# A message-passing layer: the last quad's statistics, weights and scatter taken pair by pair, and its update split three pairs to one

## The chip, the cores and the metric

The kernel runs on one core of one Trainium2 chip. The metric is device time in microseconds of one execution. Before the change the median of four runs was 577.39 us, from 576.52 to 577.80.

## The reference

One layer of a graph network on 128 graphs of 64 nodes with 128 features. Every ordered pair of nodes has a message, a three-layer network with layer norms; the messages are masked by the adjacency matrix and summed; a second network of the same form updates the node.

```python
def _mlp(x, w0, b0, g0, be0, w1, b1, g1, be1, w2, b2):
    h = relu(x @ w0 + b0);  h = _layernorm(h, g0, be0)
    h = relu(h @ w1 + b1);  h = _layernorm(h, g1, be1)
    return h @ w2 + b2
# x: (128, 64, 128), adj: (128, 64, 64) of 0 and 1, about one entry in eight set
pair_feats = concatenate([f_i, f_j], axis=-1)            # (B, P, P, 2C)
messages   = _mlp(pair_feats, msg_*) * adj[..., None]
agg        = sum(messages, axis=2)
out        = x + _mlp(concatenate([x, agg], axis=-1), upd_*)
```

## The kernel before, in words

**Edges, not node pairs.** Only the edges that the adjacency matrix has are computed. Two graphs are a *pair* (64 of them, `NP`); a pair has 2 x 640 edge slots, 10 tiles of 128 edges. Two pairs are a *quad* (32, `NQ`; 20 tiles, `QT`), and four tiles are a *chunk*, so a quad has 5 chunks (`QC`) and the whole 160 (`NCHK`). Four pairs are a *block* (16, `NB`) of 512 nodes, the unit of the node update. The last quad, 31, holds pairs 62 and 63 and chunks 155 to 159; the last block, 15, holds pairs 60 to 63, and block 14 pairs 56 to 59.

**A chunk.** `layer0` forms h on TensorE (PE) and ScalarE (ACT). `stats0` turns h on PE and takes `bn_stats` on VectorE (DVE). Layer norms are not applied to the data: their means are folded into the weights and their deviations are carried as per-edge factors. `layer1` (eight steps later, `L1`) multiplies h by the centred weights onto a bias scaled by the deviation and leaves y = relu(...) by ACT. `stats1` takes the statistics of y on DVE.

**A quad.** `var1_step` combines the statistics of 20 tiles (seven small instructions: on GpSimd, POOL, and on DVE for the last quad), `root1_of` takes the root on ACT, `inverse_of` the reciprocal on DVE. `weights(p, g)` multiplies a pair's edge-to-node marks by this factor (two instructions a pair, on POOL; for the last quad pair 62's are on DVE). `reduce(p)` is the scatter: ten products y x weights on PE that sum a pair's edges into its nodes, in the PSUM bank `ys`. In the last block the bank is taken anew for its second half.

**A block.** A `Unit` is the update of some pairs of a block. It copies the sums (`sums_out`, ysum), turns and copies them (`turn`, `turn_out`, ysumT), multiplies (`layer`), adds the bias `m0` of `bias0` and takes relu with statistics (`layer_out`, uh), turns and copies that, multiplies by u1 and adds `usdb`, the bias scaled by the deviation (`upd_shift`, one ACT instruction a pair), takes uy, turns, multiplies by u2, and ends with `finish`, one DVE instruction `uo` a pair and a store. Variances are `upd_m0` and `upd_m1`, five and seven small instructions, by POOL or by DVE. Up to block 14 a block is one unit. Block 15 is two: pairs 60, 61 and pairs 62, 63. All units' tiles of one name share one buffer (`bufs=1`), `uo`, `xo` and `m0` two.

**Order.** Every engine works through its own queue in the order in which the program issues. That order is written by hand: `at(n, place, fn, ...)` puts a call into step n at a place, and the last loop runs, for each step, the places "a", "m", then `layer1(n - 8)`, "b", `layer0`, `stats0`, "k", `stats1(n - 8)`, "x", "x1", "x2", "e0", "e1", "e". `LAST` lists the steps of the units of the last blocks. Steps of the tail: `layer1` of chunk 155 is in step 163, of chunk 159 in 167; the last scatter is in step 169.

**Lines.** L249 to L278 are the small statistics, roots and reciprocals; L567 the split of a root; L609 and L612 `layer1`; L619 `stats1`; L682 `weights`; L695 `reduce`; L721 ysum; L728 `bias0`; L734 `residual` (xo); L740 and L745 turning and copying out; L754 the units' products; L242 and L764 uh, uy and their statistics; L777 `upd_shift`; L791 uo; L794 the store.

Of the kernel before, what the change touches and what calls it, by code (L numbers as in the profile page):

```python
# [23 lines left out]
def tile_gnn(  # L24
# [245 lines left out]
    def root1(stp, v, n, name):  # L270

        sq = stp.tile([P, n], F32, name=name + "_sq")
        nc.scalar.activation(sq, v, AF.Sqrt, scale=1.0 / C, bias=eps2_c)
        return sq
# [14 lines left out]
    def edge_path(es):  # L289
# [3 lines left out]
        sp = es.enter_context(tc.tile_pool(name="sp", bufs=4))  # L293
        hp = es.enter_context(tc.tile_pool(name="hp", bufs=9))
        yp = es.enter_context(tc.tile_pool(name="yp", bufs=12))
        lp = es.enter_context(tc.tile_pool(name="lp", bufs=3))
        wp = es.enter_context(tc.tile_pool(name="wp", bufs=2))
        updp = es.enter_context(tc.tile_pool(name="upd", bufs=1))
        stp = es.enter_context(tc.tile_pool(name="stp", bufs=5))
# [22 lines left out]
        def zbank(k):  # L322
            return ps_z[k].tile([P, CH * C], F32, name=f"z{k}")
# [4 lines left out]
        def at(n, place, fn, *args):  # L328
            plan.setdefault((n, place), []).append((fn, args))
# [284 lines left out]
        def stats1(n):  # L614
# [3 lines left out]
            for t in range(CH):  # L618
                nc.vector.bn_stats(ST1[q][:, CH * c + t, :], Y[n][:, t, :])  # L619

        def var1_step(q):
            Q[q] = var1_of(stp, ST1.pop(q), V0.pop(q), QT, "m21", eng_of(q))

# [18 lines left out]
        def bias_table():  # L642

            K = 4 * QT
            part, tile_of = W.pop("part"), W["tile_of"]
            hi = const.tile([P, C], F32R, name="b1hi")
            nc.scalar.copy(hi, W["b1b"])
            lo = const.tile([P, C], F32, name="b1lo")
            nc.gpsimd.tensor_tensor(lo, W["b1b"], hi.bitcast(F32), op=ALU.subtract)
            nc.gpsimd.tensor_scalar(lo, lo, part[:, 1:2], None, op0=ALU.mult)  # L650
            mix = const.tile([P, C], F32, name="b1mix")
            nc.gpsimd.tensor_scalar(mix, hi.bitcast(F32), part[:, 0:1], None, op0=ALU.mult)
            nc.gpsimd.tensor_tensor(mix, mix, lo, op=ALU.add)
            W["b1t"] = const.tile([K, QT, C], F32R, name="b1t")
            W["b1mix"], W["tile_of"] = mix[0:K], tile_of[0:K]
# [20 lines left out]
        def weights(p, g):  # L676

            q, h = divmod(p, 2)
            if g == 0:
                WT[p] = wp.tile([P, TG, 2, N], F32, name="w")  # L680
            k = (2 * h + g) * TG
            (nc.vector if p == NP - 2 else nc.gpsimd).tensor_tensor(  # L682
                WT[p][:, :, g, :], OH[p][:, :, g * N:(g + 1) * N],
                Q[q][:, k:k + TG].unsqueeze(2).to_broadcast([P, TG, N]), op=ALU.mult)

        def reduce(p):
            b, k = divmod(p, PB)
            if k == 0 or (b == NB - 1 and k == PB // 2):
                YS[b] = ps_y.tile([P, PB, C], F32, name="ys")
            w = WT.pop(p)  # L690
            for t in range(TG):
                for g in range(2):
                    tile_no = p * 2 * TG + g * TG + t
                    y = Y[tile_no // CH][:, tile_no % CH, :]
                    nc.tensor.matmul(YS[b][g * N:(g + 1) * N, k, :], lhsT=w[:, t, g, :], rhs=y,  # L695
                                     start=(t == 0), stop=(t == TG - 1))
            if p % 2:
                for n in range(p // 2 * QC, (p // 2 + 1) * QC):
                    del Y[n]
# [12 lines left out]
        def wide(name, u):  # L712

            if name not in u.blk:
                u.blk[name] = updp.tile([P, PB, C], F32, name=name,
                                        bufs=2 if name in ("uo", "xo", "m0") else 1)
            return u.blk[name][:, u.q, :]

        def sums_out(u):
            u.ysum = wide("ysum", u)  # L720
            nc.scalar.copy(u.ysum, YS[u.b][:, u.q, :])  # L721
            if u.k0 + u.n == PB:
                del YS[u.b]

        def bias0(u):
            u.m0 = wide("m0", u)
# [46 lines left out]
        def upd_shift(u, q0, q1):  # L773
            if q0 == 0:
                u.usdb = wide("usdb", u)
            for q in range(q0, q1):
                nc.scalar.activation(u.usdb[:, q, :], W["bu1b"], AF.Copy, scale=u.sd[:, q:q + 1])  # L777

# [9 lines left out]
        def finish(u):  # L788
            o = wide("uo", u)
            for q in range(u.n):  # L790
# [16 lines left out]

        LAST = ((1, 2, 3, 3, 4, 5, 6, 6, 8, 9, 10, 11, 11, 11, 12),
                (0, 5, 6, 6, 7, 7, 8, 8, 8, 9, 9, 10, 10, 10, 11),
                (2, 2, 3, 3, 4, 4, 5, 5, 5, 6, 6, 7, 7, 7, 8),  # L810
                (1, 1, 2, 2, 3, 3, 4, 4, 4, 5, 5, 6, 6, 6, 7))
        for b in range(NB):
            o = b * CPB
# [19 lines left out]
        for b in reversed(range(NB)):  # L833
            o = b * CPB
            n = o + QC + SC

            if b < NB - 1:
                t = STEADY if b < NB - 3 else LAST[b - NB + 3]
                units = [(Unit(b, 0, PB, nc.gpsimd, ubank), n, t, 0, t[5] - 1)]
                if b == NB - 2:  # L840
                    units = [units[0][:3] + (-5, -4)]
            else:
                units = [(Unit(b, 2, 2, nc.vector, lambda: zbank(1), tbank), NCHK + L1 + 1, LAST[3], 1, 1),
                         (Unit(b, 0, 2, nc.gpsimd, lambda: zbank(0), hbank), NCHK + L1 - 1, LAST[2], 3, 3)]
            for u, n, t, m0_at, xo_at in units:
                at(n + m0_at, "m", bias0, u)
                at(n + xo_at, "e", residual, u)
                at(n + t[0], "a", sums_out, u)
                at(n + t[1], "x", turn, u, "ysum")
                at(n + t[2], "a", turn_out, u, "ysum")  # L850
                at(n + t[3], "x", lambda u: layer(u, ("xn", u0a), ("ysumT", W["w2u"])), u)
                at(n + t[4], "m", layer_out, u, "uh", "m0")
                at(n + t[4], "e", upd_m0, u)
                at(n + t[5], "x", turn, u, "uh")
                at(n + t[6], "a", turn_out, u, "uh")
                at(n + t[7], "a", upd_root0, u)
                if t is STEADY:
                    for k, q0, q1 in ((0, 0, 1), (1, 1, 2), (2, 2, PB)):
                        at(n + t[7] + k, "x", upd_shift, u, q0, q1)
                else:  # L860
                    at(n + t[7], "x", upd_shift, u, 0, u.n)
                at(n + t[8], "x", lambda u: layer(u, ("uhT", W["u1c"])), u)
                at(n + t[9], "m", layer_out, u, "uy", "usdb")
                at(n + t[9], "e", upd_m1, u)
                at(n + t[10], "x", turn, u, "uy")
                at(n + t[11], "a", turn_out, u, "uy")
                at(n + t[12], "a", upd_root1, u)
                at(n + t[12], "m", upd_inverse, u)
                at(n + t[13], "x", lambda u: layer(u, ("uyT", W["u2c"])), u)
                at(n + t[14], "m", finish, u)  # L870
        for p in range(NP):
            n = p * TG * 2 // CH
            if p > 1:
                if p > 2:
                    at(max(n - 7, p - 2), "a", distance, p)
                    at(max(n - 6, p - 2), "m", make_tp, p)
                at(n - 5, "a", node_rows, p)
                at(n - 4, "a", stack, p, 0, IR)
                for k in range(2):
                    at(n - 5 + k, "k", marks, p, k)  # L880
                    at(n - 5 + k, "k", compare, p, k)
                at(n - 3, "a", stack, p, 1, JR)
            w = p // 2 * QC + QC + L1 + p % 2
            last = p // 2 == NQ - 1
            at(w - 4, "a", node_marks, p)
            q, h = divmod(p, 2)
            for g in range(2):
                wait = h + 2 if q == NQ - 3 else h + 1 if q == NQ - 2 else 2 + (2 * h + g + 1) // 2
                at(*((NCHK + L1, "b") if last else (q * QC + QC + L1 + wait, "e1")), weights, p, g)
            at(NCHK + L1 + 1 if last else q * QC + SC - (q >= NQ - 3), "x1", reduce, p)  # L890
        for q in range(NQ):
            n = q * QC + QC if q else LEAD
            last = q == NQ - 1
            end = q * QC + QC + L1
            at(n, "e0", var0_of, q)
            at(*((n, "e1") if last else (n + 1, "b")), root_of, q)
            at(*((n + 2, "b") if last else (n + 1 if q else QC + 1, "x")), turn_root, q)
            at(n + 2 if q else QC + 2, "x" if last else "a", root_out, q)
            at(end - last, "e1", var1_step, q)
            wait = 0 if last else 1 if q == NQ - 2 else 2  # L900
            at(end + wait, "a", root1_of, q)
            at(end + wait, "m", inverse_of, q)


        for n in range(2, NCHK - L1):
# [304 lines left out]
```

## Time and profile before

| | |
|---|---|
| median of four runs | 577.39 us |
| the profiled execution | 577.28 us, span 575.5 us |
| granted TensorE clock, mean | 0.995 |
| PE busy | 550.2 us (96%) |
| DVE, ACT, POOL busy | 479.8, 476.8, 339.4 us |
| last y (chunk 159) ends on ACT | 550.92 us |
| last scatter ends on PE | 558.37 us |
| last uo ends on DVE | 571.53 us |

The profile is of one execution. A row of the timeline has the start in us from the span's start, the duration, the engine, the line, the operation, the tile written and the tiles read, and in brackets the idle time before it and what ended that. A row with "x4" is four instructions merged, and its duration runs from the first's start to the last's end. In the waits, the numbers are the total in us, how often, and the longest. In the windows, the first two numbers are the stretch and its length; then come the busy times of PE, PE's weight loads, DVE, ACT and POOL, the granted clock, the DMA share and GB/s. Matmuls with fp32 data are recorded as two instructions each, and their ends are modelled.

### The profile page before, as it was taken

The numbers are of one execution on the slowest core, as the hardware profiler recorded it, in microseconds if no ns is written. First come the engines' busy times: TensorE is split into PE (matmuls) and PEld (weight loads), VectorE is DVE, ScalarE is ACT, GpSimd is POOL, SyncE is SP. The second block draws the span as 40 slices with busy tenths as digits, with TensorE's granted clock in tenths as the row PEclk, the third lists the DMA queues.
The fourth block names the chain that finished last, engine by engine and source line by source line (L and its number), as shares of the span: only waits on it lengthen the run. The fifth ranks groups of instructions, "written<-read, shape, count | busy, mean of one in ns | idle before, by whom it ended". The sixth has DMA issues, their size and how long they took to land. (4 is left out here: it accounts for less than half of the span.)

```text
span 575.5 us, 15748 instructions
## 1 busy us (share of the span) xinstructions
PE 550.2 (96%) x5303; PEld 515.5 (90%) x5303; DVE 479.8 (83%) x1944; ACT 476.8 (83%) x1149; POOL 339.4 (59%) x898
## 2 busy tenths in 40 slices
PE   7798999999999999999999999999999999998894
PEld 5587889999999999999999999999999999988883
DVE  5768789797989989798989979798988979896686
ACT  5677979898888989898888989888898989886434
POOL 3344466665767666565767656575766656556342
PEclk9989999999999999999999999999999999999999
DMA  4454545365544555468454555555376564631201
GB/s 101 102 136 106 127 104 139 87 120 133 125 129 104 141 113 127 103 116 153 107 138 91 134 116 117 130 125 130 93 147 113 125 104 103 134 93 32 34 21 40
DMA packets 90770, 63.21 MB, mean 110 GB/s; under 512 B 57399, under 2 KB 74813, under 8 KB 90685
## 3 DMA queue, kind: packets, MB, share of 16 engines
q1 hardware_dynamic: 90396, 62.03, 48.4%
q8 instruction: 43, 0.70, 0.5%
q14 instruction: 43, 0.34, 0.2%
q10 hardware_dynamic: 288, 0.13, 0.1%
HBM read 6.82 MB, written 4.19 MB: 19 GB/s over the span
## 5 line engine op out<-in xcount | busy, mean ns | idle before, releaser
L552 DVE BATCH_NORM_STATS2 st<-hT 128x6 f32<-128x128 f32 x640 | 142.1, 285 | 36.6 <-PE hT L548 35.1
L609 PE MATMUL z<-w1c,h 128*128 128x128 f32 x1280 | 172.2, 277 | 0.0
L609 PEld LDWEIGHTS z<-w1c,h 128*128 128x128 f32 x1280 | 161.0, 192 | 8.2 <-issue 5.1
L597 ACT ACTIVATE z<-b1b,m_sd 128x128 f32<-128x128 f32 x360 | 133.5, 371 | 8.7
L619 DVE BATCH_NORM_STATS2 st<-y 128x6 f32<-128x128 f32 x640 | 137.7, 278 | 2.7 <-ACT y L612 1.4
L612 ACT ACTIVATE y<-z 128x512 f32<-128x512 f32 x160 | 94.5, 591 | 26.7 <-PE z L609 24.9
L542 ACT ACTIVATE h<-hps,b0c 128x512 f32<-128x512 f32 x160 | 109.4, 684 | 4.6 <-PE hps L539 4.4
L548 PE MATMUL hT<-ident,h 128*128 128x128 f32 x640 | 98.2, 276 | 1.6 <-DVE st L552 1.5
L682 POOL TENSOR_TENSOR w<-oh,m_q 128x320 f32<-128x320 f16 x126 | 91.9, 741 | 9.9 <-PE hT L548 5.3
L539 PE MATMUL hps<-s,abl 128*128 128x512 f32 (+3 forms) x256 | 93.5, 377 | 1.5 <-ACT h L542 0.8
L548 PEld LDWEIGHTS hT<-ident,h 128*128 128x128 f32 x640 | 76.9, 142 | 11.9 <-ACT h L542 1.3
L497 POOL CAST i<-tp 128x640 fp32r<-128x640 f16 x58 | 41.7, 718 | 66.6 <-DVE tp L488 48.7
L539 PE MATMUL hps<-s,abh 128*128 128x512 f32 (+3 forms) x256 | 79.7, 330 | 0.0
L695 PE MATMUL ys<-y,w 128*64 128x128 f32 x1280 | 76.9, 275 | 0.0
L695 PEld LDWEIGHTS ys<-y,w 128*64 128x64 f32 x1280 | 69.2, 137 | 4.2 <-issue 3.6
L249 POOL TENSOR_TENSOR m_d<-st 128x20 f32<-128x20 f32 x62 | 16.3, 262 | 91.0 <-DVE st L552 78.0
L521 DVE TENSOR_TENSOR j<-mk,cmpt 128x320 fp32r<-128x320 f32 x124 | 58.8, 474 | 3.0 <-PE mk L513 3.0
L539 PEld LDWEIGHTS hps<-s,abl 128*128 128x128 f32 x256 | 50.3, 196 | 3.6 <-ACT h L542 2.1
L482 ACT ACTIVATE d<-slot,mid 128x640 f16<-128x640 f16 x64 | 52.7, 823 | 0.0
L539 PEld LDWEIGHTS hps<-s,abh 128*128 128x128 f32 x256 | 50.5, 197 | 0.0
L473 DVE TENSOR_TENSOR abl<-mu,abh 128x512 fp32r<-128x512 f32 (+1 forms) x33 | 22.3, 675 | 31.6 <-ACT abh L467 31.1
L513 PE MATMUL mk<-tp,posall 128*128 128x320 f16 x126 | 38.3, 304 | 3.1 <-POOL posall L397 2.5
(224 smaller groups left out, 980.8 us busy)
## 6 DMA issues: line engine op xcount, KB each, us to landing
s<-i SPq DMA_DIRECT2D x124, 160.0 KB, 2.7
s<-j SPq DMA_DIRECT2D x124, 160.0 KB, 2.6
xn<-in_x_dram SPq DMA_DIRECT2D x15, 256.0 KB, 3.6
out_dram<-uo SPq DMA_DIRECT2D x15, 256.0 KB, 2.4
an<-in_adj_dram SPq DMA_DIRECT2D x16, 128.0 KB, 2.6
oh<-tp SPq DMA_TRANSPOSE x64, 3.3
xn<-in_x_dram SPq DMA_DIRECT2D x2, 128.0 KB
out_dram<-uo SPq DMA_DIRECT2D x2, 128.0 KB, 2.6
```

Of the source, the lines that this page charges most:

```text
L482: nc.scalar.activation(D[p], slot, AF.Abs, bias=blocks[b]["mid"][:, q:q + 1], scale=-1.0)
L521: nc.vector.tensor_tensor(JR[p][:, c], MK.pop((p, k))[:, 0:HC], cmpt[:, c], op=ALU.is_equal)
L539: nc.tensor.matmul(ps[:, c:c + w], lhsT=ab[:, g % 4, :], rhs=s, start=(k == 0), stop=(k == 1))
L542: nc.scalar.activation(H[n], ps, AF.Relu, bias=b0c)
L548: nc.tensor.transpose(ps[:, t, :], H[n][:, t * P:(t + 1) * P], ident)
L552: nc.vector.bn_stats(ST0[q][:, CH * c + t, :], ps[:, t, :])
L597: nc.scalar.activation(Z[n][:, t, :], W["b1b"], AF.Copy, scale=SR[q][:, k:k + 1])
L609: nc.tensor.matmul(ps[:, t, :], lhsT=h[:, t * P:(t + 1) * P], rhs=W["w1c"], start=False, stop=True, skip_group_check=True)
L612: nc.scalar.activation(Y[n], ps, AF.Relu)
L619: nc.vector.bn_stats(ST1[q][:, CH * c + t, :], Y[n][:, t, :])
L682: (nc.vector if p == NP - 2 else nc.gpsimd).tensor_tensor(WT[p][:, :, g, :], OH[p][:, :, g * N:(g + 1) * N], Q[q][:, k:k + TG].unsqueeze(2 ...
L695: nc.tensor.matmul(YS[b][g * N:(g + 1) * N, k, :], lhsT=w[:, t, g, :], rhs=y, start=(t == 0), stop=(t == TG - 1))
```

## The change

- The statistics' combination, root and reciprocal of the last quad are made for pair 62 and for pair 63 by themselves (`var1_pair`, `rstd1_pair`, `inverse_pair`, 10 columns each) and no longer for both at once. Pair 62's variance is issued in step 165, after `stats1` of chunk 157, its root and reciprocal in step 166, its weights, both on POOL, at the end of step 166, and its scatter in step 168. Pair 63's variance is issued in step 167, root and reciprocal in 168, weights in 168 (one on DVE, one on POOL), scatter in step 169, into a bank of its own (`mk`).
- Block 15's units are of three pairs (60 to 62; scatter into one bank `ys`) and of one (63). Their steps are the same as the two units' before.
- `bias0` of these units is issued five steps ahead of their beginning, in steps 163 and 164 (before: after the last weights), and `residual` up to three steps sooner.
- Block 14's `usdb` is one POOL instruction on 128x512 in place of four by ACT.
- For space, the turned roots `sdT` have two slots in place of three, and a table of the start, `b1lo`, shares the slots of `beb`.

```diff
-        lp = es.enter_context(tc.tile_pool(name="lp", bufs=3))
+        lp = es.enter_context(tc.tile_pool(name="lp", bufs=2))
...
+        def var1_pair(p):
+            q, h = divmod(p, 2)
+            k = slice(h * QT // 2, (h + 1) * QT // 2)
+            Q[q, h] = var1_of(updp, ST1[q][:, k], V0[q][:, k], QT // 2, f"p1{h}", nc.vector)
+        def rstd1_pair(p):
+            q, h = divmod(p, 2)
+            Q[q, h] = root1(updp, Q[q, h], QT // 2, f"p1{h}")
+        def inverse_pair(p):
+            q, h = divmod(p, 2)
+            Q[q, h] = inverse(updp, Q[q, h], QT // 2, f"p1{h}")
...
-            lo = const.tile([P, C], F32, name="b1lo")
+            lo = const.tile([P, C], F32, name="beb", bufs=2)
...
-            k = (2 * h + g) * TG
-            (nc.vector if p == NP - 2 else nc.gpsimd).tensor_tensor(
+            k, r = ((2 * h + g) * TG, Q[q]) if q < NQ - 1 else (g * TG, Q[q, h])
+            (nc.vector if p == NP - 1 and g == 0 else nc.gpsimd).tensor_tensor(
...
-            if k == 0 or (b == NB - 1 and k == PB // 2):
+            if p == NP - 1:
+                YS[b] = ps_k.tile([P, 512], F32, name="mk").rearrange("p (k c) -> p k c", k=PB)
+            elif k == 0:
...
+            if u.b == NB - 2:
+                nc.gpsimd.tensor_tensor(u.usdb, bc(W["bu1b"], u.n), u.sd.unsqueeze(2).to_broadcast([P, u.n, C]),
+                                        op=ALU.mult)
+                return
...
-                units = [(Unit(b, 2, 2, nc.vector, lambda: zbank(1), tbank), NCHK + L1 + 1, LAST[3], 1, 1),
-                         (Unit(b, 0, 2, nc.gpsimd, lambda: zbank(0), hbank), NCHK + L1 - 1, LAST[2], 3, 3)]
+                units = [(Unit(b, 3, 1, nc.vector, lambda: zbank(1), tbank), NCHK + L1 + 1, LAST[2],
+                          -5, -1),
+                         (Unit(b, 0, 3, nc.gpsimd, lambda: zbank(0), hbank), NCHK + L1, LAST[2],
+                          -5, 0)]
...
-            last = p // 2 == NQ - 1
+            end = NCHK + L1
...
-                at(*((NCHK + L1, "b") if last else (q * QC + QC + L1 + wait, "e1")), weights, p, g)
-            at(NCHK + L1 + 1 if last else q * QC + SC - (q >= NQ - 3), "x1", reduce, p)
+                at(*((q * QC + QC + L1 + wait, "e1") if q < NQ - 1 else
+                     (end, "b") if h else (end - 2, "e1")), weights, p, g)
+            at(q * QC + SC - (q >= NQ - 3) if q < NQ - 1 else end + h, "x1", reduce, p)
+            if q == NQ - 1:
+                at(end - 1 if h else end - 3, "e1", var1_pair, p)
+                at(end if h else end - 2, "a", rstd1_pair, p)
+                at(end if h else end - 2, "m", inverse_pair, p)
```

## The prediction

> **What bounds the kernel now.** I read the page first, then the windows, then the waits and the timeline of the last 27 us. The page says that TensorE carries the body, and the table of windows shows where that ends:
>
> ```profile
> PE 550.2 (96%) x5303; PEld 515.5 (90%) x5303; DVE 479.8 (83%) x1944; ACT 476.8 (83%) x1149; POOL 339.4 (59%) x898
> ...
> 550.00:560.00 10.00, 9.01 (x115) 8.10 (x114) 8.26 (x28) 2.79 (x7) 4.14 (x9) 1.00 0.09 28
> 560.00:575.50 15.50, 7.89 (x58) 6.44 (x56) 9.15 (x40) 6.36 (x20) 3.82 (x21) 0.91 0.13 38
> ```
>
> PE (first pair of numbers) is full up to 550 us and half idle after 560. With line numbers left aside, the two programs' queues are the same, instruction by instruction and wait by wait, up to the last quad. So only the tail can move, and there a chain through all engines sets the end. The waits of the tail name its links:
>
> ```profile
> ACT ysum L721 <- PE ys L695: 4.3, 1, 4.3
> ...
> ACT m_sq L273 <- DVE m_v L267: 2.0, 1, 2.0
> ACT um_sq L273 <- DVE um_v L267: 1.9, 1, 1.9
> ```
>
> The timeline gives the times I work with (start, duration, engine):
>
> ```profile
> 549.19 0.60 ACT L612 ACTIVATE y<-z 128x512 f32<-128x512 f32 x1 [0.53 <-PE z L609]
> 550.32 0.60 ACT L612 ACTIVATE y<-z 128x512 f32<-128x512 f32 x1 [0.53 <-PE z L609]
> 552.94 0.31 ACT L273 ACTIVATE m_sq<-m_v,eps_c 128x20 f32<-128x20 f32 x1 [2.02 <-DVE m_v L267]
> 553.30 0.37 ACT L721 COPY ysum<-ys 128x256 f32<-128x256 f32 x1
> 553.56 0.59 ACT L745 COPY ysumT<-ma 128x512 f32<-128x512 f32 x1
> 553.79 1.97 POOL L682 TENSOR_TENSOR w<-oh,m_q 128x320 f32<-128x320 f16 x2 [3.78 <-DVE m_q L278]
> 555.97 2.40 PE L695 MATMUL ys<-y,w 128*64 128x128 f32 x40
> 561.46 1.28 ACT L777 ACTIVATE usdb<-bu1b,um_sd 128x128 f32<-128x128 f32 x4
> 562.77 0.69 DVE L242 CUSTOM_DVE_ANT_0 uy<-mu,usdb 128x512 f32<-128x512 f32 x1 [0.21 <-ACT usdb L777]
> 567.82 0.17 DVE L278 RECIPROCAL um_q<-um_sq 128x2 f32<-128x2 f32 x1
> 567.90 1.12 DVE L791 SCALAR_TENSOR_TENSOR uo<-mu,um_q,xo 128x128 f32<-128x128 f32 x4
> 570.40 1.13 DVE L791 SCALAR_TENSOR_TENSOR uo<-z,um_q,xo 128x128 f32<-128x128 f32 x4
> ```
>
> To be seen: the first two rows are the last two chunks' y (158, 159), which ACT takes as soon as PE delivers them. The quad's root (m_sq) follows at 552.94, and three things hang on it: the weights, and, behind it in ACT's queue, ysum and block 14's ysumT. Both ends meet at 555.97, where the scatter of pairs 62 and 63 begins; it delivers at 558.37. The units then need 13.16 us to the end of uo at 571.53, and 3.97 us more pass to the end of the span.
>
> **First half: up to the last scatter.** The variance of pair 62 (seven DVE instructions) now stands after the statistics of chunk 157, and its root stands in ACT's queue ahead of y158 and y159. That is an added wait on a queue: ACT cannot take y158 at 549.19, and DVE's own next statistics need y158. Step by step:
> - The statistics of 157 start at 549.14 as before; two chunks took 1.64, so DVE's queue is free at 549.93. Seven instructions took 1.17 on 20 columns and 1.01 on 2 (568.94 to 569.95); for 10 columns I take 1.09, ends 1.01 and 1.17. They end at 551.02.
> - Root on ACT 551.05, y158 from 551.26, y159 from 551.74 (two in succession took 1.08 at 540.10) to 552.34: 1.4 us later than the 550.92 of before.
> - DVE: reciprocal to 551.61, statistics of 158 at 551.89, of 159 to 553.55, pair 63's variance to 554.56, its root at 554.59. Before, the quad's root started at 552.94: 1.65 late.
> - Pair 62's weights, two by POOL at 0.72 alone, end at 553.28 and its scatter at 554.7. That is early, but nothing behind it can use it: ysum (now pairs 60 to 62) stands behind root 63 in ACT's queue: 554.95, and ysumT of block 14 at 555.33 to 555.91 (a copy of 384 columns lies between the rows of 0.37 for 256 and 0.58 for 512; I take 0.48).
> - PE has block 14's eight products between this and pair 63's scatter: from 555.85, at 0.22 each, to 557.61. Pair 63's weights (DVE 0.49 to 1.01 beside POOL 1.04) are ready by 556.4 and do not bind. One pair's scatter is half of the 2.40 row: 557.61 to 558.84, where before both ended at 558.37.
>
> So 1.65 is lost, 1.17 (one scatter off the path) is won: **+0.48**.
>
> **Moved biases.** Four instructions of 2.54 leave 555.11, where nothing was waiting for DVE: uh of block 14 was ready at 558.25, and PE came to it at 560.01. Worth 0. They go to 543.86, where DVE idled 1.32 us: three at the median 0.34 fit (0.28 apart in the queue), the fourth follows the next statistics. At the dearest row, 0.82 each, the reciprocal for pairs 60 and 61 would come 1.2 late, which is the slack their weights have (550.01 for a scatter at 551.4): 0 still; without that slack, up to 1.2. The first row bearing on this is the 2.54 itself: 0.63 apart beside POOL's xo instead of 0.28. [...]
>
> **Second half: the units.** The three-pair unit (60 to 62) stands ahead of block 14's uh in PE's queue, as the two-pair one did, and adds two products of 0.22, less 0.2 for smaller copies and transposes of the last unit: block 14's uh is turned at 560.70 (before 559.99 by the same arithmetic), root 14 is at 561.82 behind uhT. Then the change of engine:
> - Block 14's scaled bias is one POOL instruction in place of four on ACT (1.28). No row shows it; the nearest is xo of 128x512 on POOL, 1.27, and the weights' 0.72 for 320 columns gives 1.15; held up as the weights of 553.79 were, 1.85. I take 1.28: 562.22 to 563.50. uy of block 14 waits for it on either engine.
> - ACT's freed time buys nothing: the unit's uhT waits for PE's product to 563.32. But POOL does the unit's five variance instructions (1.11) **behind** this: at 563.47, not at 562.65, to 564.58. Root, three scalings at 0.32, then uy of three pairs at 566.00 (before 564.98) with 0.55 (rows: 0.42 for two pairs, 0.67 for four), statistics to 567.23, POOL variance (1.36) to 568.67, root, reciprocal at 569.03 instead of 567.76. Before, POOL's own queue set that point; now the wider uy does.
> - From there DVE's queue is unchanged in kind: four uo (1.04), seven small instructions (1.00), root and reciprocal (0.4), four uo: 572.71.
>
> Run over the kernel before, the same arithmetic ends at 571.45 (row: 571.53), so the difference is 1.26, of which the second half is 0.78. [...]
>
> **Stores.** Two stores at the end as before, now of three and one pairs. An issue takes 0.37 on SP. The larger waits for three uo, 0.26 before the last, so the last store is issued 0.37 after it, +0.08. Landing took 2.6 for 128 KB and 2.4 for 256 KB: size gives nothing.
>
> **Buffers.** One spare slot fewer for the turned roots: a slot is rewritten 17 steps after its quad begins and last read at step 12; a table of the start shares a slot long read. 0; if that cover of five steps were gone, ACT would wait for PE in every quad.
>
> **Sum.** 0.48 + 0.78 + 0.08 = 1.34. The profiled execution took 577.28 (span 575.5, 1.8 around it), 0.11 under the median of 577.39; 577.39 + 1.34 = **578.7**.
>
> **Bounds.** Chains of 1.01 give -0.2, POOL at 1.15 -0.15, both together about +1.0. POOL at 1.85 gives +0.55, chains of 1.17 +0.16, together +2.05. The runs of before lie between 576.52 and 577.80, so a median of a few runs may be off by some 0.4.
>
> **Rivals.**
> - Hidden, no change that can be told (a measurement of this kernel tells about 0.2%, 1.15 us): the low ends above, with the faster issue of a one-pair unit giving some tenths back: 578.1. For it speaks that POOL and ACT idle much of the tail; against it, that every lost wait is a queue order.
> - Faster: the split pays as it reads. The place is y158: if root 62 did not hold it, the statistics would end at 551.82 as before, root 63 would start at 552.9, and the last scatter end 1.65 sooner, 557.19, 1.18 before the old one. If the units then took their old 13.16, 576.2. It decides only if the variance of 62 is through by 549.2, when y158 is ready; it starts at 549.93, so the order speaks against it.
> - Much slower: POOL's scaling is held up (1.85) and the wider uy adds: 579.4 or more.
>
> **How the numbers follow.** Forecast 0.60 (most of it above 578.5), hidden 0.20, faster 0.07, much slower 0.13. The range from 577.3 to 579.8 leaves out less than 2 in 10. Slower by over 0.2%: 0.68; within 0.2%: 0.25; faster: 0.07.
>
> **What would show it.** Right: an ACT idle of about 1.9 before the pair's root at 551, y158 right behind it; root 63 near 554.6; pair 63's scatter starting as block 14's products end, near 557.6; POOL's usdb near 1.3 with the unit's um_d just behind; the last reciprocals and uo about 1.3 later. Wrong: y158 at 549.2, or a scatter of 63 before 556.5, or the three-pair uy before 565.

## The result and the profile after

The changed kernel takes 579.18 us (median of 36 runs) where the kernel before took 577.32 beside it: a ratio of 1.0034, 95% interval 1.0024 to 1.0044, some 1.4 to 2.5 us slower. The profiled execution took 579.32 us, with a span of 577.6.

The page and the windows of the changed kernel, with the columns of before:

```profile
PE 551.3 (95%) x5303; PEld 516.2 (89%) x5303; DVE 478.4 (83%) x1951; ACT 476.2 (82%) x1146; POOL 342.1 (59%) x900
...
550.00:560.00 10.00, 9.20 (x112) 7.91 (x110) 6.71 (x35) 2.43 (x6) 5.04 (x7) 1.00 0.09 26
560.00:577.60 17.60, 8.81 (x67) 7.51 (x65) 9.50 (x43) 6.19 (x19) 5.61 (x25) 0.90 0.11 34
```

PE runs the same 5303 instructions. After 560 us there are 17.6 us where there were 15.5, of which 0.6 is a body that came later in this execution. The waits between 549 and 575 us have new names at the top:

```profile
ACT p_sq L273 <- DVE p_v L267: 5.2, 2, 2.9
...
ACT ysum L737 <- PE mk L711: 3.2, 1, 3.2
```

ACT waits twice for a pair's variance where it waited once (2.0) for the quad's. The timeline of the tail, to be read against the rows of before:

```profile
547.70 0.31 ACT L273 ACTIVATE m_sq<-m_v,eps_c 128x20 f32<-128x20 f32 x1 [1.33 <-POOL m_v L267]
...
552.21 0.30 ACT L273 ACTIVATE p_sq<-p_v,eps_c 128x10 f32<-128x10 f32 x1 [2.93 <-DVE p_v L267]
552.41 1.07 ACT L612 ACTIVATE y<-z 128x512 f32<-128x512 f32 x2
...
555.74 0.30 ACT L273 ACTIVATE p_sq<-p_v,eps_c 128x10 f32<-128x10 f32 x1 [2.26 <-DVE p_v L267]
555.95 0.46 ACT L737 COPY ysum<-ys 128x384 f32<-128x384 f32 x1
556.31 0.59 ACT L760 COPY ysumT<-ma 128x512 f32<-128x512 f32 x1
...
558.73 1.31 PE L711 MATMUL mk<-y,w 128*64 128x128 f32 x20
...
563.50 1.04 POOL L792 TENSOR_TENSOR usdb<-bu1b,um_sd 128x512 f32<-128x512 f32 x1 [1.88 <-ACT um_sd L259]
...
567.06 0.56 DVE L242 CUSTOM_DVE_ANT_0 uy<-z,usdb 128x384 f32<-128x384 f32 x1
...
573.07 1.13 DVE L810 SCALAR_TENSOR_TENSOR uo<-z,um_q,xo 128x128 f32<-128x128 f32 x4 [0.27 <-issue]
```

To be seen: pair 62's root after 2.93 of idle and both last y right behind it (one row, 1.07 for two); root 63, then ysum, then block 14's ysumT in ACT's queue; the last scatter at 558.73; and, in the last row, 0.27 us in which DVE waited for nothing that the profile shows.

**A ruler.** The body ahead of the tail does not repeat exactly: the first product of chunk 155 (L606) starts between 542.33 and 543.80 us in the executions compared here. So all marks below are counted from that product. Two kernels with the same tail then agree to 0.02 us. "Tail" is the time from this product to the end of the last uo; the change made it 2.07 longer (28.47 to 30.54), and what follows the last uo 0.57 shorter (3.97 to 3.40). Spans are printed to 0.1 us, so the last column holds to about 0.05.

| kernel | root of 60, 61 | last scatter ends | last uo ends (tail) | span ends |
|---|---|---|---|---|
| before | 3.44 | 15.31 | 28.47 | 32.44 |
| after | 4.04 | 16.38 | 30.54 | 33.94 |
| e1, biases back | 3.44 | 15.79 | 29.92 | 33.33 |
| e2, block 14's usdb on ACT | 4.02 | 16.35 | 30.49 | 33.85 |
| e3, before with biases moved | 3.68 | 15.31 | 28.48 | 32.48 |
| e4, before with the buffers | 3.46 | 15.31 | 28.48 | 32.50 |
| f4, e1 with units of two and two | 3.44 | 15.65 | 29.15 | 32.62 |
| f5, e1 with root 62 behind y159 | 3.45 | 16.02 | 30.17 | 33.57 |
| f6, f4 and f5, block 14 sooner | 3.44 | 14.83 | 28.32 | 31.61 |
| f8, before, block 14 sooner | 3.45 | 14.57 | 27.72 | 31.69 |
| f9, before with seven memsets | 3.44 | 15.31 | 28.81 | 32.05 |
| f10, f8 with nine memsets | 3.46 | 14.58 | 27.74 | 31.76 |

### The profile page after: what moved, and what is told of

It reads as the page before. It is cut to its first block, busy times and chain, and to the rows that moved or that the text cites. A ratio compares the mean times of both kernels' runs of the same rounds, so it can differ in the third digit from the quotient of the medians.

```text
span 577.6 us, 15756 instructions
## 1 busy us (share of the span) xinstructions
PE 551.3 (95%) x5303; PEld 516.2 (89%) x5303; DVE 478.4 (83%) x1951; ACT 476.2 (82%) x1146; POOL 342.1 (59%) x900
## 5 line engine op out<-in xcount | busy, mean ns | idle before, releaser
L696 POOL TENSOR_TENSOR w<-oh,m_q 128x320 f32<-128x320 f16 x124 | 90.1, 738 | 6.1 <-PE hT L548 5.3
```

The source lines that it names most:

```text
L696: (nc.vector if p == NP - 1 and g == 0 else nc.gpsimd).tensor_tensor(WT[p][:, :, g, :], OH[p][:, :, g * N:(g + 1) * N], r[:, k:k + TG].uns ...
```

## The experiments

**e1: the biases back.** The changed kernel with `bias0` of the units where it stood in the queue before.

```diff
-                          -5, -1),
+                          1, -1),
...
-                          -5, 0)]
+                          2, 0)]
```

> The changed kernel with the last units' four biases back behind the last weights, all else as changed. Measure: the tail, from the first product of chunk 155 on TensorE to the end of the last uo; 28.47 us before, 30.54 us after the change. [...]

Tail 29.92, so the moved biases cost 0.62; ratio to before 1.0018 (1.0001 to 1.0034). Of it 0.59 lies ahead of the last scatter (16.38 to 15.79), and already in the root of pairs 60 and 61 (4.04 to 3.44). The rows of the changed kernel show how:

```profile
544.39 0.86 DVE L743 SCALAR_TENSOR_TENSOR m<-c2u,deg,ub0b 128x128 f32<-128x128 f32 x3
544.39 0.42 POOL L252 TENSOR_SCALAR um_d<-um_d 128x4 f32<-128x4 f32 x1
544.89 0.42 POOL L253 TENSOR_TENSOR um<-um_d,um_s 128x4 f32<-128x4 f32 x1
...
546.58 0.34 DVE L743 SCALAR_TENSOR_TENSOR m<-c2u,deg,ub0b 128x128 f32<-128x128 f32 x1
546.62 0.43 POOL L252 TENSOR_SCALAR m_d<-m_d 128x20 f32<-128x20 f32 x1
```

The same POOL instructions in e1, with DVE free of biases:

```profile
543.20 0.22 POOL L252 TENSOR_SCALAR um_d<-um_d 128x4 f32<-128x4 f32 x1
543.50 0.20 POOL L253 TENSOR_TENSOR um<-um_d,um_s 128x4 f32<-128x4 f32 x1
...
545.00 0.27 POOL L252 TENSOR_SCALAR m_d<-m_d 128x20 f32<-128x20 f32 x1
...
545.91 0.31 ACT L273 ACTIVATE m_sq<-m_v,eps_c 128x20 f32<-128x20 f32 x1 [0.74 <-POOL m_v L267]
```

Three small POOL statistics lose 0.20, 0.22 and 0.16 beside a bias: 0.58 of the 0.60 by which the root is late. The second and the third of them end 0.06 and 0.13 after the bias beside them; what makes them slow, no run here shows. This chain on POOL ends in the root of pairs 60 and 61 (m_sq: 547.70 in the changed kernel, 545.91 in e1), behind which ACT takes y156. The statistics of y156 then start on DVE 4.86 after chunk 155's product and not 4.27, and DVE works on from there without a gap into pair 62's variance.

**e3: the same move in the kernel before.**

```diff
-... NCHK + L1 + 1, LAST[3], 1, 1),
+... NCHK + L1 + 1, LAST[3], -5, 1),
...
-... NCHK + L1 - 1, LAST[2], 3, 3)]
+... NCHK + L1 - 1, LAST[2], -4, 3)]
```

> The kernel before with nothing changed but the four biases moved forward to steps 163 and 164. Theory: GpSimd's small statistics beside them go from 0.22 to 0.42 us, the root of pairs 60 and 61 is 0.6 late, and because chunk 156's y stands behind that root, part of it, 0.2 to 0.4 us, reaches the end: tail 28.7 to 28.9 us. Rival (the prediction's reading, all in the slack): 28.47, and the 2.54 us of biases that leave the stretch after the weights bring nothing either.

Tail 28.48: nothing, though the root does come 0.24 later. My theory missed, the rival held; ratio 1.0000 (0.9980 to 1.0021). Before, DVE idles ahead of the statistics of y159, and a chain that is a little late still meets them. With the split, DVE goes straight from the statistics of chunk 157 into pair 62's variance, and nothing is there to take up the delay. First y159's statistics in the kernel before, then, in the changed one, the first instruction of pair 62's variance, which has no idle ahead of it:

```profile
550.95 0.87 DVE L619 BATCH_NORM_STATS2 st<-y 128x6 f32<-128x128 f32 x4 [0.17 <-ACT y L612]
```

```profile
551.12 0.15 DVE L265 TENSOR_SCALAR p_v<-m 128x10 f32<-128x10 f32 x1
```

This run has two biases beside the first chain and not three, so its delay is also smaller. A delay of the full 0.6 in the kernel before was not tried; as the idle there is 0.17 and 0.24 were taken up, an estimated 0.3 to 0.4 of it would have reached the end.

**e2: block 14's scaled bias back on ACT.**

```diff
-            if u.b == NB - 2:
-                nc.gpsimd.tensor_tensor(u.usdb, bc(W["bu1b"], u.n), ...)
-                return
```

> The changed kernel with block 14's scaled bias again as four instructions on ScalarE, all else as changed. Theory (GpSimd's instruction holds the three-pair unit's variance behind it): GpSimd's um_d of the three-pair unit starts about 0.5 us earlier against block 14's root, the three-pair uy too, and the tail is 0.4 to 0.5 shorter, about 30.1 us. Rival (ScalarE is as full, so the four instructions hold its own queue instead): no change, 30.5, or longer.

Tail 30.49, 0.05 less: my theory missed, the rival held; ratio 1.0023 (1.0006 to 1.0041). The rows of e2:

```profile
563.36 0.20 POOL L249 TENSOR_TENSOR um_d<-uh_st 128x3 f32<-128x3 f32 x1 [2.38 <-DVE uh_st L779]
...
564.20 0.69 DVE L242 CUSTOM_DVE_ANT_0 uy<-mu,usdb 128x512 f32<-128x512 f32 x1 [0.33 <-PE hT L755]
...
564.99 0.99 ACT L792 ACTIVATE usdb<-bu1b,um_sd 128x128 f32<-128x128 f32 x3 [0.19 <-DVE uy L242]
...
566.43 0.56 DVE L242 CUSTOM_DVE_ANT_0 uy<-z,usdb 128x384 f32<-128x384 f32 x1
```

Counted from chunk 155's product, the three-pair unit's usdb is ready for its uy sooner (it starts at 21.94, against 22.32), but its uy starts at 23.38 against 23.40: DVE is still at work on block 14's uy, its statistics and the small unit's variance. POOL's instruction did hold the unit's variance behind it; nobody waited for that. Nor did block 14's uy wait for its scaled bias: in e2 as in the changed kernel it stood 0.33 idle until PE let it go.

```profile
564.84 0.69 DVE L242 CUSTOM_DVE_ANT_0 uy<-mu,usdb 128x512 f32<-128x512 f32 x1 [0.33 <-PE hT L755]
```

**e4: the buffers alone**, in the kernel before.

```diff
-        lp = es.enter_context(tc.tile_pool(name="lp", bufs=3))
+        lp = es.enter_context(tc.tile_pool(name="lp", bufs=2))
...
-            lo = const.tile([P, C], F32, name="b1lo")
+            lo = const.tile([P, C], F32, name="beb", bufs=2)
```

> The kernel before with nothing changed but the buffers: two slots for the turned roots, and the start's table in a shared slot. In the profile after, chunk 155's first product stood at 543.66 us, 0.60 later than before. Theory: that is scatter between executions; here chunk 155 starts at 543.06 within 0.4 and the time is the same within 0.1%. Rival (the buffers' new places cost something in every quad): 543.6 or later, time 0.1% longer.

Tail 28.48, ratio 0.9986 (0.9966 to 1.0006): nothing. Chunk 155's product stood at 543.80, where the rival and not my theory had put it, but the time was no longer. And e1, f5 and f6, which have these buffers too, have it at 542.33 to 542.49, so its place is scatter between executions.

**f4: units of two and two.** e1 with the split kept and the units as before; both scatters of the last quad go into the bank `mk`. With the units, their residuals are back in their old steps too.

```diff
...
-Unit(b, 3, 1, ...), NCHK + L1 + 1, LAST[2], 1, -1),
-Unit(b, 0, 3, ...), NCHK + L1, LAST[2], 2, 0)]
+Unit(b, 2, 2, ...), NCHK + L1 + 1, LAST[3], 1, 1),
+Unit(b, 0, 2, ...), NCHK + L1 - 1, LAST[2], 3, 3)]
```

> The measure is the tail, from the first product of chunk 155 on PE to the end of the last uo on DVE: 28.47 us before, 30.54 after, 29.92 after with the units' biases where they were. This kernel is the last of these with the units of two and two pairs again (their steps as before; the pair split of statistics, weights and scatter stays, both scatters into the second bank). Theory: the part of the slowdown behind the last scatter, +1.0, comes from the three-pair unit: its two extra products ahead of block 14's uh, its wider uy and statistics, and the 0.27 idle before the last uo. Then the second half falls from 14.13 to about 13.2, the last scatter still ends near 15.7 (15.79), and the tail is 28.8 to 29.05; time 577.8. Rival: the second half is longer because GpSimd scales block 14's bias and because more instructions stand in DVE's queue; then it stays near 14.1 and the tail at 29.8. The idle of 0.27 before uo: absent, if it belongs to the units of three and one; present, if it belongs to the place in DVE's instruction stream.

Tail 29.15, 0.77 less than e1: 0.14 ahead of the last scatter (a shorter ysum and two turns for three), 0.63 behind it. So the uneven units cost 0.77; the residuals' place has no visible part in it, for the biases beside them end at 15.19 in e1 and in f4. Ratio 1.0017 (0.9999 to 1.0036). The idle of 0.27 ahead of the last uo was still there, so it does not belong to the units: my theory was wrong on that, and the tail came out above what it had said (28.8 to 29.05).

**f9: seven memsets.** In every kernel with that idle, the uo that suffers it is the 2112th instruction that the trace records of DVE, its waits and branches counted; before, it is the 2105th. (The page leaves those out: it has 1951 and 1944 instructions on DVE.) So the kernel before gets seven more DVE instructions, at its start. It was executed once.

```diff
+        pad = const.tile([P, 8], F32, name="pad")
+        for k in range(7):
+            nc.vector.memset(pad[:, k:k + 1], 0.0)
```

> The kernel before with seven small memsets of a scratch tile put on DVE at the start of the program, so that the first uo of the units is the 2112th instruction of DVE's stream, as it is after the change (before: the 2105th). Theory: the idle of 0.27 that nothing in the profile explains belongs to the place in the stream, not to the units or to what the instruction waits for; it appears here ahead of the first of the last four uo, and the tail is 28.73 to 28.75. Rival: it belongs to something else in the changed kernel, such as the two chains of small statistics; then none appears and the tail is 28.47.

The idle appears, in a kernel with nothing else changed:

```profile
570.61 0.17 DVE L278 RECIPROCAL um_q<-um_sq 128x2 f32<-128x2 f32 x1 [0.36 <-ACT um_sq L273]
571.04 1.12 DVE L791 SCALAR_TENSOR_TENSOR uo<-z,um_q,xo 128x128 f32<-128x128 f32 x4 [0.26 <-issue]
```

Before, this uo started 0.08 after the reciprocal did, here 0.43: the tail is 28.81, 0.34 longer. But from the last uo to the end of the span it is 3.24 in place of 3.97, so that all in all this execution ends 0.39 sooner after chunk 155's product (577.12 us in all, which as a single time tells nothing). The place in the stream, which a change moves by adding any instruction, was worth 0.34 of the tail here, as much as most steps of the sum. The profile counts 43 packets of 16 KB on one instruction queue (0.70 MB), while a second instruction queue carried packets of 8 KB. That the idle has to do with one of these packets no run here shows.

**f5: root 62 behind the last y.** e1 with pair 62's root, reciprocal and weights one step later, so that y158 and y159 no longer wait for them.

```diff
-                at(end if h else end - 2, "a", rstd1_pair, p)
-                at(end if h else end - 2, "m", inverse_pair, p)
+                at(*((end, "a") if h else (end - 1, "b")), rstd1_pair, p)
+                at(*((end, "m") if h else (end - 1, "b")), inverse_pair, p)
...
-                     (end, "b") if h else (end - 2, "e1")), weights, p, g)
+                     (end, "b") if h else (end - 1, "e1")), weights, p, g)
```

> After with the units' biases where they were (tail 29.92), and pair 62's root, reciprocal and weights one step later, so that the root stands behind the last two chunks' y in ACT's queue and no longer ahead of them. Rival, as the prediction put it: the root ahead of y158 is what loses the first half; y158 is then taken as PE delivers it (6.1 after chunk 155's product, not 8.2), the statistics end 0.8 sooner, root 63 starts near 10.75 (11.49), and the tail falls by the same 0.75 to about 29.2. Theory: root 63 starts near 10.75, but ysum of pairs 60 to 62 now waits for pair 62's scatter (weights end near 10.4, scatter near 11.6) and starts near 11.7 again; block 14's ysumT and products stand behind it, pair 63's scatter ends at 15.75 and the tail stays at 29.9; time 578.2.

y158 is at 6.14 after chunk 155's product, as before the change (e1: 8.16), and the tail is **longer** by 0.25; ratio 1.0023 (1.0010 to 1.0037). Root 63 comes only 0.27 sooner (11.49 to 11.22), for pair 62's weights on POOL now meet pair 63's variance on DVE, and ysum waits for pair 62's scatter:

```profile
552.13 0.70 DVE L250 TENSOR_TENSOR p_s<-st 128x10 f32<-128x10 f32 x1
```

```profile
551.38 1.42 POOL L696 TENSOR_TENSOR w<-oh,p_q 128x320 f32<-128x320 f16 x2 [2.08 <-DVE p_q L278]
...
552.41 1.74 PE L711 MATMUL ys<-y,w 128*64 128x128 f32 x20
...
554.25 0.48 ACT L737 COPY ysum<-ys 128x384 f32<-128x384 f32 x1 [0.39 <-PE ys L711]
```

L250 took 0.17 for the same columns in e1; here it ends as POOL's weights do, 552.83 and 552.80. So holding y158 was the visible delay, but taking it away frees nothing: a pair's scatter that must come before ysum is next.

**f6, f7, f8: block 14's turned sums sooner.** In f6 (f4 and f5 together) and in f8 (the kernel before), block 14's ysumT, products and uh stand one step sooner, so that PE has its eight products ahead of the last scatter and not behind its wait:

```diff
-                (0, 5, 6, 6, 7, 7, 8, 8, 8, 9, 9, 10, 10, 10, 11),
+                (0, 4, 5, 5, 6, 7, 8, 8, 8, 9, 9, 10, 10, 10, 11),
```

> The pair split with units of two and two, the biases where they were, pair 62's root behind the last y, and block 14's turned sums one step sooner, so that its ysumT stands ahead of root 63 in ACT's queue and its eight products run on PE while PE waits for the weights. Theory: what kept the split from paying is queue order. Root 63 near 10.75, the last scatter ends near 14.1 (15.31 before, 16.38 after), second half 13.1 to 13.3, tail 27.3 to 27.7, time about 576.5, 0.15% under before. Rival: a unit step behind the scatter takes the gain back, as block 14's uh then meets other work on DVE: second half near 14, tail 28.2 or more, time 577.2 or more.

> The kernel before with one line changed: the steps of block 14's unit from its turned sums on are one or two sooner, so that its eight products stand on PE ahead of the quad's scatter and no longer between its halves' copies; nothing is split. Theory: PE's idle time in front of the last scatter takes the eight products, so the tail falls by 0.7 to 0.9 without any of the change: last scatter ends near 14.6 (15.31), tail 27.6 to 27.8, time 576.5. Rival: the last scatter waits for the weights anyway and the units' own chain fills the rest; tail 28.3 or more, time 577.2.

> The kernel before with one line changed: block 14's turned sums are copied, and its products and uh made, one step sooner, so that its ysumT stands ahead of y159 in ACT's queue and its eight products stand on PE ahead of the last quad's scatter; all later steps of block 14 stand where they were, and nothing is split. Theory: what PE has to do between chunk 159's product and the last scatter is the bound of the first half (60 and 61's scatter 2.40, block 14's turn 0.6 and products 1.8, the last scatter 2.4 to 2.6: from 7.1 to 14.5), and any order that keeps PE supplied reaches it, split or not. Last scatter ends at 14.5 to 14.7 (15.31 before), second half 13.0 to 13.3 as before, tail 27.5 to 27.9 (28.47), time about 576.6. Rival: block 14's uh, taken sooner on DVE, pushes the biases and then the units; second half 13.8, tail 28.4, time 577.3.

f7 moved the later steps too, and there block 14's uhT is copied ahead of the turn of uh, so its update is another computation; of it I read only that the last scatter ends at 14.58, and its time (ratio 0.9974, 0.9956 to 0.9991) says nothing of this layer. f8 is the same idea with the later steps left in place: the last scatter ends at 14.57, the tail is 27.72, 0.75 under before, and the second half is unchanged (13.15). With the split (f6) the last scatter ends at 14.83 and the tail is 28.32. Neither side of its expectation holds there: the scatter came sooner than before but not at 14.1, as root 63 was at 11.24 and not 10.75 (as in f5, pair 63's L250 on DVE took 0.70 beside pair 62's weights on POOL); and the second half is 13.49, neither 13.1 to 13.3 nor near 14, which is 13.15 and the 0.34 of f9's idle. To the end of the span f6 and f8 are alike (31.61 and 31.69). PE's windows say why another order of this work can do little more. From where chunk 159's products leave PE to the end of the last scatter, first in the kernel before, then in f8, then in f6 (stretch, length, busy time of PE):

```profile
550.10:558.37 8.27, 7.75 (x104) 6.85 (x102) 7.38 (x24) 1.77 (x4) 3.44 (x4) 1.00 0.10 32
```

```profile
550.46:557.98 7.52, 7.52 (x104) 6.77 (x102) 6.64 (x27) 1.66 (x4) 2.75 (x6) 1.00 0.12 35
```

```profile
549.56:557.32 7.76, 7.76 (x104) 6.73 (x102) 6.95 (x33) 1.94 (x5) 3.22 (x6) 1.00 0.11 34
```

The same 104 matmul records; in f8 and f6 PE has no gap. Before, the stretch was 8.27, so a reordering that leaves these records behind chunk 159 could win about 0.75 there, and one line of f8 wins it in the tail without a split. In times, f8 has 576.55 us beside 577.49, ratio 0.9981 (0.9963 to 1.0000), at the edge of what can be told; f6 has 1.0007 (0.9992 to 1.0021), no change.

**f10: f8 with nine memsets**, so that the 2112th instruction is the last reciprocal, where DVE waits anyway.

> The kernel that has block 14's turned sums one step sooner (tail 27.72, then 3.97 us from the end of the last uo to the end of the span), with nine small memsets on DVE at the start of the program. So far every kernel whose first of the last four uo is the 2112th instruction of DVE's stream idled 0.27 there and then needed only 3.24 to 3.47 us after the last uo, its last store landing in 1.8 to 2.1 us; every kernel in which it is the 2105th (or 2104th) needed 3.97 to 4.03, its last store landing in 2.6 to 2.7, whatever the store's size. With nine more, the 2112th instruction is the last unit's reciprocal, where DVE waits 0.36 for ACT anyway. Theory: the place in the stream sets both, so that the idle falls into that wait and is not added: tail 27.7 to 27.8, no idle without a cause ahead of uo, 3.2 to 3.5 us after the last uo, and from chunk 155's product to the end of the span 31.0 to 31.25 (31.69); time about 576.0. Rival one: the idle is added to the wait, tail 28.05. Rival two: the 3.97 has to do with something else, and stays.

The tail is 27.74 and the idle is gone:

```profile
569.57 0.17 DVE L278 RECIPROCAL um_q<-um_sq 128x2 f32<-128x2 f32 x1 [0.36 <-ACT um_sq L273]
569.66 1.12 DVE L791 SCALAR_TENSOR_TENSOR uo<-z,um_q,xo 128x128 f32<-128x128 f32 x4
```

So it can be hidden in a wait. But 4.02 us follow the last uo (its last store landed in 2.7), and rival two holds for these: the short end came only with the visible idle, and why is open. Ratio 1.0002 (0.9987 to 1.0018): with f8's tail, but not f8's 0.9981, so that whole times do not confirm the 0.75 of the tail.

## Why the prediction was right, and where its steps were not

**The sum.** 1.34 was predicted, the runs say 1.4 to 2.5. From chunk 155's product to the end of the span the profiles differ by 1.50, so the size came out; but it is made of other terms than mine: 1.07 up to the last scatter (0.48 predicted), 1.00 behind it (0.78) and -0.57 behind the last uo (0.08). That the sum fits is in part luck: the 0.62 of the moved biases, which I had put at 0, and the 0.57 at the end, which I had not foreseen, nearly cancel.

**First half, +0.48: right, step by step.** Less 0.60 for the later body and 0.60 for the biases, the rows of the changed kernel are: root 62 at 551.01 (predicted 551.05), y158 at 551.21 (551.26), root 63 at 554.54 (554.59), ysum at 554.75 (554.95), pair 63's scatter from 557.53 (557.61). The biases back (e1), the last scatter ends 0.48 later than before. One sign was misworked: from the end of y157 to pair 62's root my own times give 2.4 of idle and not 1.9, and 2.93 less the biases' 0.60 is 2.33. What the runs add: 0.14 of the 0.48 are the uneven units' copies and turns (f4). The other 0.34 do not go by moving root 62 alone (f5); they go in f6, which moves root 62 and feeds PE sooner, and feeding PE sooner was not tried alone with the split.

**Moved biases, 0: this step failed.** They cost 0.62. I had costed them against the weights of pairs 60 and 61, with their slack, and taken what the overlap costs as DVE's loss. It was POOL's loss, 0.58 in three instructions, and who waited for POOL's chain was ACT, with y156 behind the root, and then every statistic up to pair 62's variance, which the same change had put on the path. The row that I named for this cost, the four biases beside xo (three of them start 0.73 apart, not 0.63), was the right kind of row, read on the wrong engine. In the kernel before, a root late by 0.24 cost nothing (e3): it is the split that let the whole delay through.

**Second half, +0.78: right size, wrong composition.** Measured behind the last scatter: 13.16 to 14.16, +1.00. Of this 0.63 are the uneven units (f4), 0.34 the place in DVE's stream (f9) and 0.03 the moved biases (e1: 14.13). The scaled bias on POOL, whose queue I had let carry the delay, has 0.02 (e2: 14.14), less than these marks can tell. Its own duration, 1.04, was under the row of 1.27 that I took (the xo instruction) and under the 1.15 that the weights' row gave. Two steps failed. "uy of block 14 waits for it on either engine": in the changed kernel and in e2 it waited for PE. And "behind this": the next thing ready was DVE's queue, not POOL's. The idle ahead of the last uo is no term of my sum at all.

**Stores, +0.08: this step failed.** The last store was issued 0.24 after the last uo where it had been 0.03, but what follows the last uo fell by 0.57, and this store (64 KB) landed in 1.9 and not 2.6. It is not the size: f9 stores 128 KB and landed it in 1.9, with 3.24 behind the last uo. The short end comes with the idle of 0.27; what makes it is open.

**Buffers, 0:** right (e4).

**The rivals.** "Faster" had its place, y158, and f5 tried exactly that: y158 was free and the tail went up by 0.25. "Much slower" needed POOL's scaling held to 1.85; it took 1.04. "Hidden" fell with the ratio, whose interval (1.0024 to 1.0044) lies above 0.2%.

## What to carry to other kernels

Before splitting work to start it sooner, add up what the busiest engine still has to do from that point on: here PE had 7.5 us of it in 8.27, and moving block 14's ready products ahead of a wait took as much off the tail as the split could have. An instruction moved into an engine's idle time is not free if it slows another engine that is in a chain then: here POOL's statistics of 0.20 to 0.27 took 0.42 or 0.43 beside a bias on DVE, and the tail grew by 0.62. Ask who waits for the other engine. And compare tails from a common mark: 0.05 us can be told there, where whole times tell about one, and then a gain of 0.75 in the tail stays unconfirmed in the time.

## What the runs showed of the hardware

- Small POOL instructions of 0.20 to 0.27 took 0.42 or 0.43 beside a bias on DVE (e1 and the changed kernel), and a DVE one of 0.17 took 0.70 beside POOL's weights (e1 and f5): it went both ways. Not every overlap costs that much: in e3 two small POOL instructions that overlapped a bias took 0.20 and 0.25, alone 0.20 and 0.23.
- An idle of 0.26 to 0.27 on DVE ahead of the 2112th instruction of its stream, in all seven kernels in which that was a uo with no wait of its own. In f10, where it is a reciprocal that waits 0.36 for ACT, no idle is added.
- After the last uo, 3.24 to 3.47 us in the kernels with this idle, whether the last store had 64 or 128 KB, and 3.97 to 4.02 in those without, all with 128 KB. The cause stays open.
